# A four-layer graph network on one core: weight generation in six single-bank PSUM places, y copied by halves of nodes, planes loaded one step earlier

## The chip, the cores and the metric

The kernel runs on one core of one Trainium2 chip. The metric is device time in microseconds (us) for one execution; the lower the better. Engine names are those of the profile: PE is TensorE's matmul, PEld its weight load, DVE is VectorE, ACT is ScalarE, POOL is GpSimd, SP is SyncE. Here SP does nothing but start transfers (DMAs); POOL and ACT start some too.

## The reference, cut to what matters

`x` is (8, 2048, 64), `adj` a row-normalised 2048 x 2048 matrix. Four layers each add their result to x after a layer norm and a ReLU. The change lies in and just behind layer 0, a graph convolution whose weights are made for each node from a 16-long embedding:

```python
w = jnp.einsum('nd,dkio->nkio', embedding, weight)   # D = 16, K = 3, 64 x 64 weights for each of 2048 nodes
b = jnp.einsum('nd,do->no', embedding, bias)
As = [I, A, 2.0 * (A @ A) - I]
x_g = jnp.einsum('knm,bmc->bnkc', jnp.stack(As, 0), x)
out = jnp.einsum('bnki,nkio->bno', x_g, w) + b
...
x = x + _L0_gnn_ref(h, adj, ...)          # layer 0
x = x + _L1_gnn_ref(relu(layernorm(x)))   # layer 1: three steps of v -> W2 relu(W1 [v, A v] + b1) + b2
...                                       # layer 2: A x and a linear map; layer 3: attention, done here as a mean
```

## The kernel before, in words

**Stages.** The adjacency matrix is loaded and kept in SBUF (`BT`), and layer 0's terms A h and A A h are formed by matmuls (`bv` in the profile). Then A's chunks are given up for space, except three of sixteen. What follows is the group stage, from about 280 us to 530 us of the span. Behind it A is loaded again (`load_again`, from a bf16 copy), and layers 1 to 3 run, again as `bv` matmuls.

**The group stage** goes over 16 groups `g` of 128 nodes, each in six steps `i`. In step `i` of group `g` the kernel writes, in this order:

- `make_w(g + 1, i)` (line 1160): a sixth of the next group's weights. Sixteen matmuls with 64 contraction rows each (eight pieces `o` of 128 columns, for two row halves `r`) fill two PSUM tiles; then DVE copies the first tile and ACT the second into `w` in SBUF. Group 0's weights are made ahead of the loop, with three `bv` matmuls of the last term of A A h behind each of the six steps.
- `apply_w(g, i)` (line 1246): a sixth of the products y of group g. Steps 0 and 3 open a tile `yb` of two banks and issue 64 short matmuls into it; steps 1, 2, 4 and 5 issue 32 each. Behind steps 2 and 5 the tile is copied to `ys`, half by ACT and half by DVE. There is one `yb` place, so the 64 matmuls of step 0 or 3 write where the previous half of y has just been copied out. After step 5 POOL starts four stores `yD<-ys`.
- `beside(g, i)` (line 1334): pieces of layer 1's first input, for 512 nodes in each round of four groups. `x1_pieces` (line 1276) is a generator with ten pieces; `beside_at` (line 1315) names the ten steps of a round in which they are issued. The last five are: two half copies to planes `pl` (ACT), the second with a store `hp<-pl` from POOL; two transposing loads `pt<-hp` from SP (`load_planes`, line 228); and two joins `gT<-pt` by ACT. One tile `pt` is held.
- `beside_first` (line 1320): some loads for the next round.

At the start of each group SP issues `load_group` for the next one (three transfers, 1 MB), which wait until the group before has released the tile.

**Order.** In this part `nc.on` holds all five engines (line 1055): each engine takes its instructions in the order in which the program writes them, and an instruction that waits holds up all behind it on that engine.

**PSUM.** It has eight banks of 512 fp32 columns. In the loop two pools share them: `psumg` with two `gen` tiles of two banks, and `psumy` with one `genx` tile of two banks and one `yb` tile of two banks. `gen_tile` takes every third tile from `genx`, so there are three generation places of two banks, used in turn, two in each step. Ahead of the loop, while four banks hold other sums, only the two `gen` tiles exist.

**Behind the loop.** `first_operand` makes the three first operands of layer 1 from the joined planes (`bn_u`), and `first_step` (line 1578) runs A times them with four running sums in two tiles of two banks. For m = 0 to 11 it goes over all four sums; then for each sum `nb` it issues the last four chunks, scales the sum on DVE (`g<-bv,crow`), and behind the third one maps the first two results (`bn`), whose PSUM tile takes the place of one of the two sum tiles.

All matmul calls and most others pass through one wrapper, so the profile gives line 67 for nearly everything; groups are told apart by tile names. `w<-gen` is the copy of generated weights, `gen<-E,wg` the generating matmul, `yb<-w,t` the 64 and `yb<-w,tt` the 32 matmuls of y, `ys<-yb` y's copies.

Of the kernel before, what the change touches and what calls it, by code (L numbers as in the profile page):

```python
# [8 lines left out]
F32 = mybir.dt.float32  # L9
# [66 lines left out]
def uniform_path(  # L76
# [42 lines left out]
    psums = [pro.enter_context(tc.tile_pool(name="psump", bufs=1, space=bass.MemoryType.PSUM))]  # L119
# [30 lines left out]
    def bank(tag, name):  # L150
        return psums[-1].tile([P, 512], F32, tag=tag, name=name)
# [221 lines left out]
    def to_feat(h, out, name):  # L373
        pt = transposed(lambda t: h[:, t, :], name)
        nc.scalar.copy(out, pt.rearrange("p t n -> p (t n)"))
        return out
# [305 lines left out]
    ps = bank("b1", f"bv_{nm}")  # L682
    for m in range(NCH):
        if m in (2, 7, 12):
            go_back(1 + m // 5)
        for i in range(2):
            nc.tensor.matmul(
                ps, hls[1][m // 4][i][:, m % 4, :], bt(m)[:, 3 * 512:],
                start=(m == 0 and i == 0), stop=(m == NCH - 1 and i == 1),
# [8 lines left out]
        name="psumt", bufs=2, space=bass.MemoryType.PSUM, reuse_waits="tile"  # L698
# [77 lines left out]
    two = (slice(0, C), slice(C, P))  # L776
# [269 lines left out]
    for m in range(NCH):  # L1046
        i = m if m < 9 else m + 3
# [8 lines left out]
    for n, (kind, p) in enumerate(rounds):  # L1056
        own = kind == "a"
        for nb in range(NB if n + 1 < len(rounds) else 0):
            i = 4 * n + nb
# [8 lines left out]
            if i < 19:  # L1068
                load_ahead(i + 1)
            act(i, -1)  # L1070
            t = product(
                hl_of[kind, p], nb, nm, term(1 if own else 2, f"t{2 - own}T_{nm}"), crows_t[nb],
                fill=fill,
            )
# [8 lines left out]
    psums.pop()  # L1083
    pgs, pls = ExitStack(), ExitStack()
    psg = pgs.enter_context(tc.tile_pool(
        name="psumg", bufs=2, space=bass.MemoryType.PSUM, reuse_waits="tile"
    ))
    psgs.append(psg)
    psl = pls.enter_context(tc.tile_pool(
        name="psuml", bufs=1, space=bass.MemoryType.PSUM, reuse_waits="tile"  # L1090
    ))
    multiply = nc.tensor.matmul
# [35 lines left out]
    wg = wp.tile([P, 2, K * D * C], F32R, tag="A", name="wg")  # L1128
    w1s = [wp.tile([P, P, C], F32, tag="BC"[i], name=f"w1_{i}") for i in range(2)]
    w2 = wp.tile([P, P, C // 2], F32, tag="D", name="w2")  # L1130
# [18 lines left out]
        for hf in range(2):  # L1149
            nc.sync.dma_start(t2s[g % 2][two[hf]], TD[:, 2, :, cs].rearrange("b i n -> i b n"))  # L1150

    gens, moved, pys = [], {}, []

    def gen_tile(g, i, h):
        pool = psg if not pys or len(gens) % 3 < 2 else psums[-1]
        tag = "gen" if pool is psg else "genx"
        gens.append(pool.tile([P, 2, 512], F32, tag=tag, name=f"gen_{g}_{i}_{h}"))
        return gens[-1]

    def make_w(g, i):  # L1160

        e = es_[g]
        ps = [gen_tile(g, i, h) for h in range(2)]
        k2 = i > 3
        n0 = 8 * (i - 4 if k2 else i)
        for o in range(8):
            q, n = divmod(n0 + o, D // 2 if k2 else D)
            at = 2 * D * C * k2 + n * P
            wide = 1 + (g % 4 == 1 and o % 4 < 3)
            for r in range(2):  # L1170
                rs = two[r]
                multiply(
                    ps[r].rearrange("p a f -> p (a f)")[:, o * P:(o + wide) * P],
                    wg[rs, q, at:at + P], e[rs, None, :].to_broadcast([2 * D * 2, wide, P]),
                    start=True, stop=True,
                )
        w, per = (w2, D) if k2 else (w1s[g % 2], 2 * D)
        for h in range(2):
            src = ps[h].rearrange("p a f -> p (a f)").rearrange("p (o n) -> p n o", o=8)
            moved[h] = (nc.vector.tensor_copy, nc.scalar.copy)[h](  # L1180
                w[:, :, per * h + n0:per * h + n0 + 8], src
            )

    load_e(0)
    load_e(1)
# [2 lines left out]
    for k in range(6):  # L1188
        make_w(0, k)
        nb = 1 + k // 2  # L1190
        for q in range(3 * (k % 2), 3 * (k % 2) + 3):
            m, i = order_l[NCH - KEEP + q // 2], q % 2
            multiply(
                lasts[nb], hl[m // 4][i][:, m % 4, :], bt(m)[:, nb * 512:(nb + 1) * 512],
                start=False, stop=(q == 5),
# [16 lines left out]
        name="psumy", bufs=1, space=bass.MemoryType.PSUM, reuse_waits="tile"  # L1212
# [3 lines left out]
    yps, yss = {}, {}  # L1216

    def apply_k(g, u, k):

        T, s_ = divmod(u, 2)  # L1220
        yp, tt, t2 = yps[g, T], tts[g % 2], t2s[g % 2]
        wa = w1s[g % 2].rearrange("p (j q) o -> p q j o", j=4)
        wb = w2.rearrange("p (j q) o -> p q j o", j=4)

        def one(hf, t, par, lhsT, rhs, start, stop):

            q_ = D * hf + 8 * T + 4 * s_ + t
            at = (2 * hf + s_) * P
            multiply(
                yp[32 * t:32 * t + 32, par, at:at + P],  # L1230
                lhsT.rearrange("p b (j q) -> p (b j) q", j=4)[:, :, q_], rhs[:, q_],
                start=start, stop=stop,
            )

        for hf in range(2):
            if k == 0:
                for par in range(2):
                    for t in range(4):
                        one(hf, t, par, tt, wa[:, :, :, 32 * par:32 * par + 32], False,
                            hf == 1 and s_ == 1)  # L1240
                continue
            for t in range(4):
                for par in range(2):
                    one(hf, t, par, t2[two[par]], wb[two[par]], hf == 0 and s_ == 0, False)

    def apply_w(g, i):

        T = i // 3
        if i in (0, 3):
            pool, tag = (psg, "gen") if (g, T) == (NCH - 1, 1) else (psums[-1], "yb")  # L1250
            yps[g, T] = pool.tile([P, 2, 512], F32, tag=tag, name=f"yb_{g}_{T}")
        u = 2 * T
        if i % 3 == 0:
            apply_k(g, u, 1)
            apply_k(g, u + 1, 1)
        else:
            apply_k(g, u + i % 3 - 1, 0)
        if i in (2, 5):
            if T == 0:
                yss[g] = typ0.tile([P, 2, 4, 4 * C], F32, tag="ys", name=f"ys_{g}", bufs=2)  # L1260
            ys, yp = yss[g], yps[g, T]
            for par in range(2):
                (nc.scalar.copy, nc.vector.tensor_copy)[par](
                    ys[:, :, 2 * T:2 * T + 2, :].rearrange(
                        "p h s (j r o) -> p h (s j) r o", j=4, r=2
                    )[:, :, :, par],
                    yp[:, par].rearrange("p (h x o) -> p h x o", h=2, o=32),
                )
            if T == 1:
                nb, t = divmod(g, 4)  # L1270
                yr = ys.rearrange("(x j) h u f -> j x h u f", j=4)
                yd = yD[nb][:, :, :, t].rearrange("t b (j h u) c -> j (t b) h u c", h=2, j=4)
                for j in range(4):
                    nc.gpsimd.dma_start(yd[j], yr[j][:, :, :, j * C:(j + 1) * C])

    def x1_pieces(p, nb, acc, yt, bn):
# [35 lines left out]
                    nc.scalar.copy(out_[:, 0:1], ivt)  # L1312
            yield

    beside_at = [(1, i) for i in (0, 1, 3, 4)] + [(2, i) for i in (0, 1, 3)] + [
        (3, i) for i in (0, 3, 4)
    ]
    firsts_ = []

# [42 lines left out]
    for g in range(NCH):  # L1362
# [28 lines left out]
        name="psum", bufs=2, space=bass.MemoryType.PSUM, reuse_waits="tile"  # L1391
# [186 lines left out]
    def first_step(hl, gT, crow_of, g_new, hl_new, nm, map_two, maps_two, finish_two, scale, add):  # L1578

        two_ = [psums[-1].tile([P, 2, 512], F32, tag="big", name=f"bv2_{i}") for i in range(2)]  # L1580
        sums = [two_[nb // 2][:, nb % 2] for nb in range(NB)]

        def crow(nb):
            crow_of[nb] = load_crow(nb, f"{nm}_{nb}")

        crow(0)
        crow(1)
        for m in range(3 * NB):
            for nb in range(NB):
                chunks(sums[nb], hl, nb, (m,))  # L1590
            if m == KEEP:
                x1_add(last_z.append)
                widen(10, nc.vector.tensor_copy)
                go_on()
                widen(11, nc.vector.tensor_copy)
                go_on()
                for k in range(12, NCH):
                    widen(k, nc.scalar.copy if k in by_act else nc.vector.tensor_copy)
            if m == 2 * NB:
                map_two(0)  # L1600
        ops[0][1].append(to_feat(last_z[0], feat(0, "gT_1_0_3"), "gT_1_0_3"))
        first_operand(3)
        x1_load(1, 0)
        for _ in range(3):
            test_load()
        for nb in range(NB):
            chunks(sums[nb], hl, nb, range(3 * NB, NCH))
            scale(sums[nb], nb)
            if nb < 2:
                crow(nb + 2)  # L1610
            if nb == 2:
                map_two(2)
                finish_two(0, maps_two(0))
            add(nb)
            go_on()
        x1_load(1, 1)
        nc.on = ("gpsimd",)
        first_done.append(products[-1])
        later.extend((x1_behind, x1_behind))

        def put_off():
            ps = maps_two(2)
            return lambda: finish_two(2, ps)

        carry.append(put_off)
        return hl_new, g_new
# [741 lines left out]
```

## Time and profile before

| | |
|---|---|
| time, median of 6 runs | 1152.16 us (1149.37 to 1155.42) |
| profiled execution: time / span | 1148.28 us / 1146.2 us |
| busy share: PE, PEld, DVE, ACT, POOL | 94%, 76%, 56%, 37%, 24% |
| granted TensorE clock, mean | 0.984 |
| `w<-gen` copies, 128 x 1024: DVE x96, ACT x96 | 1221 ns, 1025 ns each |
| `ys<-yb` copies, 128 x 512: DVE x32, ACT x32 | 691 ns, 586 ns each |
| group stage: first `gen` matmul, first `bv` matmul behind it | 279.65 us, 532.22 us |

The two times of the profiled execution differ by 2.1 us, which lie around the span. A line of the timeline gives start, duration, engine, operation, tiles and, in brackets, how long the engine had been idle and who released it. Matmuls overlap, and their durations hold their pipeline; what a burst of matmuls costs is better read from its start to the start of the burst behind it.

### The profile page before, as it was taken

The numbers are of one execution on the slowest core, as the hardware profiler recorded it, in microseconds if no ns is written. First come the engines' busy times: TensorE is split into PE (matmuls) and PEld (weight loads), VectorE is DVE, ScalarE is ACT, GpSimd is POOL, SyncE is SP. The second block draws the span as 40 slices with busy tenths as digits, with TensorE's granted clock in tenths as the row PEclk, the third lists the DMA queues.
The fourth block names the chain that finished last, engine by engine and source line by source line (L and its number), as shares of the span: only waits on it lengthen the run. The fifth ranks groups of instructions, "written<-read, shape, count | busy, mean of one in ns | idle before, by whom it ended". The sixth has DMA issues, their size and how long they took to land.

```text
span 1146.2 us, 27894 instructions
## 1 busy us (share of the span) xinstructions
PE 1081.1 (94%) x12030; PEld 865.6 (76%) x12030; DVE 637.3 (56%) x1096; ACT 429.1 (37%) x594; POOL 276.0 (24%) x313
## 2 busy tenths in 40 slices
PE   9999999999999999997898988999799999899996
PEld 7778788887788888886676765776577777688875
DVE  5555434411656666663586567557755644556575
ACT  5814322431445555554434432353244323211110
POOL 6514100100122313131123343134313300332121
PEclk9999999999999999999999999999899999899998
DMA  9936567555544454548697467736883663431432
GB/s 350 388 113 171 176 180 178 171 156 180 129 97 119 107 127 116 129 127 283 131 196 205 112 174 193 170 108 153 200 177 102 183 131 84 151 108 47 141 112 77
DMA packets 160196, 179.28 MB, mean 156 GB/s; under 512 B 63048, under 2 KB 114888, under 8 KB 157504
## 3 DMA queue, kind: packets, MB, share of 16 engines
q1 hardware_dynamic: 139744, 116.99, 41.5%
q0 software_dynamic: 13760, 45.21, 11.9%
q10 hardware_dynamic: 6560, 15.21, 4.1%
q8 instruction: 96, 1.57, 0.6%
q14 instruction: 36, 0.29, 0.1%
HBM read 111.81 MB, written 53.22 MB: 144 GB/s over the span
## 4 chain that ended last, share of the span: by engine, by line
PE 63%; DMA 11%; DVE 9%; issue 5%; ACT 5%; POOL 3%; SPq 2%; ACTq 0%; DVEq 0%; POOLq 0%
PE bv L67 28%; PE gen L67 5%; PE yb L67 5%; PE bv_2a L67 3%; PE bv_3a L67 3%; DMA yD<-ys 2%; PE bv_1a L67 2%; PE bv_2b L67 2%; PE bv_1b L67 2%; PE bv_0b L67 2%; PE bn L67 2%; PE bv_3b L67 2%; DVE z L67 2%; DVE ys L67 2%; ACT w L67 2%
## 5 line engine op out<-in xcount | busy, mean ns | idle before, releaser
L67 POOL TENSOR_TENSOR rstd<-var,mhalf 128x8 f32<-128x8 f32 x64 | 109.7, 1715 | 302.0 <-DVE var L67 299.2
L67 DVE COPY w<-gen 128x1024 f32<-128x1024 f32 x96 | 117.2, 1221 | 78.8 <-PE gen L67 78.8
L67 ACT COPY w<-gen 128x1024 f32<-128x1024 f32 x96 | 98.4, 1025 | 122.2 <-PE gen L67 122.2
L67 PE MATMUL gen<-E,wg 64*128 64x128 f32 (+1 forms) x1536 | 123.4, 282 | 1.3 <-ACT w L67 1.3
L67 PEld LDWEIGHTS gen<-E,wg 64*128 64x128 f32 x1536 | 104.7, 186 | 23.0 <-issue 8.4
L67 ACT ACTIVATE sq<-z 128x512 f32<-128x512 f32 x64 | 40.5, 632 | 197.1 <-DVE z L67 143.8
L67 POOL DMA_DIRECT2D yD<-ys x64 | 37.3, 590 | 176.2 <-DVE ys L67 174.5
L67 PE MATMUL yb<-w,tt 128*32 128x128 f32 x2048 | 73.7, 283 | 3.9 <-issue 3.9
L67 PE MATMUL bv<-BT_C,H 128*128 128x512 f32 x192 | 77.1, 401 | 0.0
L67 PE MATMUL bv<-BT_B,L 128*128 128x512 f32 x192 | 76.2, 397 | 0.2 <-DVE L L67 0.2
L67 PE MATMUL bv<-BT_B,H 128*128 128x512 f32 x192 | 75.9, 395 | 0.0
L67 PE MATMUL bv<-BT_C,L 128*128 128x512 f32 x192 | 75.8, 395 | 0.0
L67 DVE SCALAR_TENSOR_TENSOR z<-z,rstd 128x512 f32<-128x512 f32 x64 | 44.7, 698 | 50.5 <-POOL rstd L67 49.9
L67 PEld LDWEIGHTS yb<-w,tt 128*32 128x32 f32 x2048 | 59.5, 166 | 9.3 <-issue 4.9
L67 PE MATMUL bv<-BT,H 128*128 128x512 f32 x144 | 59.4, 413 | 3.2 <-ACT H L67 3.2
L67 DVE TENSOR_TENSOR g<-bv,crow 128x512 f32<-128x512 f32 x48 | 32.9, 686 | 52.4 <-PE bv L67 52.4
L67 PE MATMUL bv<-BT_A,L 128*128 128x512 f32 x144 | 57.0, 396 | 1.1 <-DVE L L67 1.1
L67 PE MATMUL bv<-BT,L 128*128 128x512 f32 x144 | 57.3, 398 | 0.5 <-DVE L L67 0.5
L67 PE MATMUL bv<-BT_A,H 128*128 128x512 f32 x144 | 56.6, 393 | 0.0
L67 DVE SCALAR_TENSOR_TENSOR junk<-mt,cols,st 128x512 uint8<-128x512 bf16 x64 | 47.7, 746 | 10.4 <-DMA mt<-MD 10.0
L67 POOL TENSOR_TENSOR acc<-acc,wl 128x512 f32<-128x512 f32 x16 | 21.5, 1342 | 126.5 <-DVE z L67 125.8
L67 DVE SCALAR_TENSOR_TENSOR z<-mean,acc 128x256 f32<-128x256 f32 x112 | 50.2, 486 | 1.4 <-DMA hs<-z 0.5
(271 smaller groups left out, 2381.5 us busy)
## 6 DMA issues: line engine op xcount, KB each, us to landing
BT<-in_adj_dram POOLq DMA_DIRECT2D x16, 1024.0 KB, 12.3
crow<-crowD SPq DMA_DIRECT2D x64, 256.0 KB, 3.5
st<-in_adj_dram SPq DMA_DIRECT2D x64, 256.0 KB, 4.5
MD<-md ACTq DMA_DIRECT2D x16, 512.0 KB, 4.2
tt<-TD SPq DMA_DIRECT2D x16, 512.0 KB, 4.4
t<-TD SPq DMA_DIRECT2D x32, 256.0 KB, 5.8
xs<-acc POOLq DMA_DIRECT2D x32, 256.0 KB, 3.1
acc<-xs SPq DMA_DIRECT2D x32, 256.0 KB, 3.6
```

The source lines that it names most:

```text
L67: made = f(*args, **how)
```

## The change

It has four parts.

1. The generation tiles are of one bank instead of two: four `gen` and two `genx` places. `make_w` takes its eight pieces in two halves `a` of four; behind each half it copies two tiles of 512 columns, one by DVE and one by ACT. Ahead of the loop there are four places instead of two.
2. In groups with `g % 2 == 1` instead of `g % 4 == 1`, three of four generating matmuls stream 256 columns instead of 128; the second 128 columns are overwritten by the next matmul.
3. y is copied by halves of nodes (`h`), ACT the first and DVE the second, where each engine took one bank (`par`) before. For the very last half of y, two single-bank tiles stand in for one of two banks, and there are four copies of 256 columns. In `first_step` the sums 0 and 2 now share a tile, and 1 and 3, where 0 and 1 did, and 2 and 3.
4. The ten pieces are issued at other steps: `load_planes` in step 4 of a round's third group instead of step 0 of its fourth, and the two joins in steps 1 and 3 instead of 3 and 4.

```diff
@@ psumg
-        name="psumg", bufs=2, space=bass.MemoryType.PSUM, reuse_waits="tile"
+        name="psumg", bufs=4, space=bass.MemoryType.PSUM, reuse_waits="tile"
@@ gen_tile, make_w
-    def gen_tile(g, i, h):
-        pool = psg if not pys or len(gens) % 3 < 2 else psums[-1]
-        tag = "gen" if pool is psg else "genx"
-        gens.append(pool.tile([P, 2, 512], F32, tag=tag, name=f"gen_{g}_{i}_{h}"))
+    def gen_tile(g, i, h, a):
+        pool = psg if not pys or len(gens) % 6 < 4 else psums[-1]
+        tag, bufs = ("gen", 4) if pool is psg else ("genx", 2)
+        gens.append(pool.tile([P, 512], F32, tag=tag, name=f"gen_{g}_{i}_{h}_{a}", bufs=bufs))
...
-        ps = [gen_tile(g, i, h) for h in range(2)]
-        for o in range(8):
-            q, n = divmod(n0 + o, D // 2 if k2 else D)
-            wide = 1 + (g % 4 == 1 and o % 4 < 3)
+        for a in range(2):
+            ps = [gen_tile(g, i, h, a) for h in range(2)]
+            for o in range(4):
+                q, n = divmod(n0 + 4 * a + o, D // 2 if k2 else D)
+                wide = 1 + (g % 2 == 1 and o < 3)
...
+            for h in range(2):
+                o0 = per * h + n0 + 4 * a
+                (nc.vector.tensor_copy, nc.scalar.copy)[h](
+                    w[:, :, o0:o0 + 4], ps[h].rearrange("p (o n) -> p n o", o=4)
                 )
@@ apply_w
-            for par in range(2):
-                (nc.scalar.copy, nc.vector.tensor_copy)[par](
-                    ys[:, :, 2 * T:2 * T + 2, :].rearrange(
-                        "p h s (j r o) -> p h (s j) r o", j=4, r=2
-                    )[:, :, :, par],
-                    yp[:, par].rearrange("p (h x o) -> p h x o", h=2, o=32),
-                )
+            for h in range(2):
+                copy = (nc.scalar.copy, nc.vector.tensor_copy)[h]
+                to = ys[:, h, 2 * T:2 * T + 2, :].rearrange("p s (j r o) -> p r (s j) o", j=4, r=2)
+                if len(yp) == 3:
+                    copy(to, yp[2].rearrange("p r (h x o) -> p h r x o", h=2, o=32)[:, h])
+                    continue
+                for r in range(2):
+                    copy(to[:, r], yp[r].rearrange("p (h x o) -> p h x o", h=2, o=32)[:, h])
@@ beside_at
-    beside_at = [(1, i) for i in (0, 1, 3, 4)] + [(2, i) for i in (0, 1, 3)] + [
-        (3, i) for i in (0, 3, 4)
+    beside_at = [(1, i) for i in (0, 1, 3, 4)] + [(2, i) for i in (0, 1, 3, 4)] + [
+        (3, i) for i in (1, 3)
     ]
@@ first_step
-        sums = [two_[nb // 2][:, nb % 2] for nb in range(NB)]
+        sums = [two_[nb % 2][:, nb // 2] for nb in range(NB)]
```

More of the change, by code (lines that the diff above doesn't have):

```diff
@@ L1150, in load_group @@
             nc.sync.dma_start(t2s[g % 2][two[hf]], TD[:, 2, :, cs].rearrange("b i n -> i b n"))
-    gens, moved, pys = [], {}, []
-    def gen_tile(g, i, h):
-        pool = psg if not pys or len(gens) % 3 < 2 else psums[-1]
-        tag = "gen" if pool is psg else "genx"
-        gens.append(pool.tile([P, 2, 512], F32, tag=tag, name=f"gen_{g}_{i}_{h}"))
+    gens, pys = [], []
+    def gen_tile(g, i, h, a):
+        pool = psg if not pys or len(gens) % 6 < 4 else psums[-1]
+        tag, bufs = ("gen", 4) if pool is psg else ("genx", 2)
+        gens.append(pool.tile([P, 512], F32, tag=tag, name=f"gen_{g}_{i}_{h}_{a}", bufs=bufs))
         return gens[-1]
@@ L1162, in make_w @@
         e = es_[g]
-        ps = [gen_tile(g, i, h) for h in range(2)]
         k2 = i > 3
         n0 = 8 * (i - 4 if k2 else i)
-        for o in range(8):
-            q, n = divmod(n0 + o, D // 2 if k2 else D)
-            at = 2 * D * C * k2 + n * P
-            wide = 1 + (g % 4 == 1 and o % 4 < 3)
[L1170 to L1175, printed above, removed]
-                )
[L1177 to L1181, printed above, removed]
-            )
+        w, per = (w2, D) if k2 else (w1s[g % 2], 2 * D)
+        for a in range(2):
+            ps = [gen_tile(g, i, h, a) for h in range(2)]
+            for o in range(4):
+                q, n = divmod(n0 + 4 * a + o, D // 2 if k2 else D)
+                at = 2 * D * C * k2 + n * P
+                wide = 1 + (g % 2 == 1 and o < 3)
+                for r in range(2):
+                    rs = two[r]
+                    multiply(
+                        ps[r][:, o * P:(o + wide) * P],
+                        wg[rs, q, at:at + P], e[rs, None, :].to_broadcast([2 * D * 2, wide, P]),
+                        start=True, stop=True,
+                    )
+            for h in range(2):
+                o0 = per * h + n0 + 4 * a
+                (nc.vector.tensor_copy, nc.scalar.copy)[h](
+                    w[:, :, o0:o0 + 4], ps[h].rearrange("p (o n) -> p n o", o=4)
+                )
     load_e(0)
@@ L1229, in one @@
             multiply(
-                yp[32 * t:32 * t + 32, par, at:at + P],
+                yp[par][32 * t:32 * t + 32, at:at + P],
                 lhsT.rearrange("p b (j q) -> p (b j) q", j=4)[:, :, q_], rhs[:, q_],
@@ L1249, in apply_w @@
         if i in (0, 3):
-            pool, tag = (psg, "gen") if (g, T) == (NCH - 1, 1) else (psums[-1], "yb")
-            yps[g, T] = pool.tile([P, 2, 512], F32, tag=tag, name=f"yb_{g}_{T}")
+            if (g, T) == (NCH - 1, 1):
+                yps[g, T] = [
+                    psg.tile([P, 512], F32, tag="gen", name=f"yb_{g}_{T}_{par}") for par in range(2)
+                ]
+            else:
+                yb = psums[-1].tile([P, 2, 512], F32, tag="yb", name=f"yb_{g}_{T}", bufs=1)
+                yps[g, T] = [yb[:, 0], yb[:, 1], yb]
         u = 2 * T
@@ L1261, in apply_w @@
             ys, yp = yss[g], yps[g, T]
-            for par in range(2):
-                (nc.scalar.copy, nc.vector.tensor_copy)[par](
-                    ys[:, :, 2 * T:2 * T + 2, :].rearrange(
-                        "p h s (j r o) -> p h (s j) r o", j=4, r=2
-                    )[:, :, :, par],
-                    yp[:, par].rearrange("p (h x o) -> p h x o", h=2, o=32),
-                )
+            for h in range(2):
[4 more added lines that the diff above has]
+                    continue
+                for r in range(2):
+                    copy(to[:, r], yp[r].rearrange("p (h x o) -> p h x o", h=2, o=32)[:, h])
             if T == 1:
```

## The prediction

> **What bounds the kernel now.** The page comes first: PE is busy for 94% of the span, and the rows of the groups show both copy engines idle most of the time before a copy, waiting for PE. So the question is what PE's own bursts wait for. The timeline of a plain stretch of the group stage (half of group 10) answers it:
>
> ```profile
> 439.95 1.31 PE L67 MATMUL gen<-E,wg 64*128 64x128 f32 x16
> 440.07 0.58 ACT L67 COPY ys<-yb 128x512 f32<-128x512 f32 x1
> 440.69 0.69 DVE L67 COPY ys<-yb 128x512 f32<-128x512 f32 x1 [0.58 <-ACT ys L67]
> 441.43 1.25 PE L67 MATMUL yb<-w,t 64*32 64x128 f32 x64 [0.17 <-DVE ys L67]
> 442.62 1.11 PE L67 MATMUL gen<-E,wg 64*128 64x128 f32 x16
> 443.66 1.15 PE L67 MATMUL yb<-w,tt 128*32 128x128 f32 x32
> 443.76 1.22 DVE L67 COPY w<-gen 128x1024 f32<-128x1024 f32 x1 [0.66 <-PE gen L67]
> 444.73 1.41 PE L67 MATMUL gen<-E,wg 64*128 64x128 f32 x16
> 446.08 1.14 PE L67 MATMUL yb<-w,tt 128*32 128x128 f32 x32
> 447.15 0.33 PE L67 MATMUL gen<-E,wg 64*128 64x128 f32 x1
> ```
>
> From start to start, a generation burst takes 1.04 us where nothing holds it (442.62 to 443.66), 1.35 at 444.73 and 1.48 at 439.95. The burst of 444.73 writes the place that DVE empties from 443.76 to 444.98: 0.25 us late, the missing 0.31 with a semaphore's delay. The 1.48 has another cause: the 64 y matmuls behind it need `yb` empty, and its copies run one after the other, ACT to 440.65, DVE to 441.38, PE at 441.43. A half group is thus 1.19 (64 y) + 1.04 + 1.07 + 1.35 + 1.07 + 1.48 = 7.20 us, a group 14.41 (starts of the 64 at 324.48 and 338.89). In a doubled group the free burst is 1.08 (354.50 to 355.58) and the group 14.59 (353.31 to 367.90).
>
> Then the chain that ended last, at the end of the stage:
>
> ```profile
> 516.01 11.87 DMA pt<-hp
> ...
> 528.54 0.58 ACT ys L67
> ...
> 529.14 0.52 DVE ys L67
> ...
> 529.75 0.69 DVE L_u L67
> ```
>
> The planes, issued at 514.74 behind seven 512 KB loads of A, hold ACT (8.26 us idle before the first join); behind ACT wait the last y copy and the first operands, so PE has no `bv` matmul before 532.22, though y's matmuls began their last burst at 521.77.
>
> **The change part by part.**
>
> *Six places.* With places of one bank taken in order, half a burst needs the copy of three halves before. At 444.73 that copy would be long over, so 1.35 becomes 1.04: 0.31 a half group. The new copies have 512 columns; I price them by y's, which are that size and also from PSUM: 691 ns on DVE, 586 on ACT. DVE then has 12 x 0.69 + 2 x 0.69 = 9.7 us in a plain group, and 12.3 in the group with the most pieces (11.3 busy now, + 12 x 0.69 - 6 x 1.22 = 1.0), against a period of 13.8. The first half's copy starts half a burst earlier, so y's copies find DVE free as now. Bounds: no gain if a small copy costs 1.0 us (rival d); 0.4 a half if every burst gets the 0.97 that the weight loads take.
>
> *Doubling.* The free burst costs 0.04 more; the one ahead of y's wait nothing. Eight groups instead of four.
>
> Plain periods become 14.41 - 0.62 = 13.79, doubled ones 13.79 + 4 x 0.04 = 13.95. Fifteen periods generate: now 11 x 14.41 + 4 x 14.59 = 216.9; after 7 x 13.79 + 8 x 13.95 = 208.1. **Sum: -8.8** (-5 to -12).
>
> *Ahead of the loop* six bursts with three `bv` matmuls each take 2.32 (284.27 to 286.60 is 2.33), and PE waits 0.21 for ACT's copy with the burst stretched besides. Free, it is 1.04 + 3 x 0.23 = 1.73; DVE needs as much (four copies of 0.69 and one scaling of 0.68 in two bursts: 1.72 each). With both this close I take 1.87: **-2.7** (-1.5 to -3.5).
>
> *y by halves.* I count nothing. The old copies read different banks of one tile and yet ran one after the other. That this is a rule of reading one PSUM tile, not of what is written, is shown where ACT and DVE take different parts of a tile `wt`:
>
> ```profile
> 165.41 0.75 DVE L67 TENSOR_SCALAR wst<-wt,rows 128x512 f32<-128x512 f32 x1 [4.57 <-DMA MD<-md]
> 166.20 0.59 ACT L67 CAST whq<-wt 128x512 fp32r<-128x512 f32 x1 [2.69 <-DVE wst L67]
> ```
>
> ACT needs nothing that DVE makes there, and starts 0.04 us behind it. The new halves still share the tile, so 1.48 stays. The four small copies of the very last half overlap in part; that is 0.2 us and not counted. Bounds: 0, and -0.44 a half group if they do run together (a rival). The Trainium skill (PSUM — Partial Sum Buffer, "PSUM bank collisions raise a hardware error") has it that two engines may not be in one bank and partition quadrant at once, two readers included, but may be in different banks. The trace is stricter than that on the old copies (0.58 us idle across banks); on the new ones, which both read both banks, page and trace agree on no overlap.
>
> *Planes earlier.* Two transposing loads move on SP ahead of `load_group` (three transfers) in the rounds' third groups, and of `load_again` (seven) at the end. SP will stand there for the store `hp<-pl` (issued 508.23, 2.5 us to landing), then 2 x 1.25 us of issue; `load_group` has a period of 14 us to land in 4.4 to 5.9, and A's first reloaded chunk is used 5.5 us into `bv`: both hidden, 2.5 us if not. On ACT the joins pass ahead of two steps of copies; landing by 4.2 us (median of `pt`) puts the first at 15.4 to 16 us from its group's start, the join's place is at 17: no stall; with 7.3 us as at 398.12 some 1.4 us, which three half-burst places cover.
>
> At the end the planes land near 516 instead of 527.9. From 513.73 to 523.27 PE does y (its 2.94 us pause with no releaser kept); then two operands (2.05), the third behind the first one's release (`L_u`, about 2.5 behind y), 1.1 more: `bv` starts 13.1 us from 513.73, now 18.5. **-5.5** (-2 to -8.5, the pause gone too).
>
> *Sums in other pairs.* The same tile rule shows here:
>
> ```profile
> 562.58 0.50 PE L67 MATMUL bv<-BT_C,H_u 128*128 128x512 f32 x1 [0.78 <-DVE g L67]
> 567.37 1.11 PE L67 MATMUL bn<-wl,g 64*64 64x64 f32 x64
> 568.89 0.68 DVE L67 TENSOR_TENSOR g<-bv,crow 128x512 f32<-128x512 f32 x1
> 569.63 0.51 PE L67 MATMUL bv<-BT_C,H_u 128*128 128x512 f32 x1 [1.16 <-DVE g L67]
> ```
>
> Sums 1 and 3 wait for the scaling of 0 and 2. Those waits go (-0.8, -1.2). But `bn` takes the tile of sums 0 and 2 and must now wait for the scaling at 568.89, which DVE reaches late because a test waits 1.40 for its transfer: `bn` moves 2.2 us back, and with it PE's last sum and the operands for the next step. **+0.5** (-0.8 to +1.5).
>
> **Sum:** -8.8 - 2.7 - 5.5 + 0.5 = -16.5. From the profiled 1148.28 us that is 1131.8; that execution lay 3.9 under the median, so from 1152.16 it is **1135.7**.
>
> **Rivals.**
> (a) *y's copies do run together.* For it: all written parts are separate blocks now, interleaved before. Against: `wst`/`whq` above. The 64 matmuls would wait only for the 1.04 burst: 2 x 15 x 0.44 = -13.2, and doubling costs 0.04 more in 16 bursts: about -13 further, 1122.5.
> (b) *Only the generation gains*: planes land late behind other traffic (11.9 us once already), `bn` loses 1.5, the start gives 1.5: -8.8 - 1.5 + 1.5 = about -9: 1143.
> (c) *No change*: PE is held for the copies as before, if half bursts are released together. Against: each tile has its own two copies. 1152.
> (d) *Slower: DVE becomes the bound.* 384 copies replace 192, and a fixed part is paid twice; runs of four elements are written instead of eight. In four periods DVE has 48 copies of d, eight y copies (5.5) and 4.3 us of pieces (4 x 0.68, 0.75, 0.85 in the timeline of groups 4 to 7); this reaches the present 57.6 us at d = 1.0. At 1.1 the period is 15.65, +18.6 over 15, less 5.5 at the end: 1165. Against: 691 ns for the same size.
>
> **How the numbers follow.** Chances: forecast 0.57, (a) 0.16, (b) 0.12, (c) 0.05, (d) 0.10. A difference of 0.3% (3.5 us) is about what can be told here. Faster: 0.57 + 0.16 + 0.12 = 0.85; same 0.05; slower 0.10. The forecast's own range by its terms is 1128 to 1144; with (a) at the low end and (b) at the high one I give 1119 to 1147, which leaves out (c), (d) and the far side of (a).
>
> **What would show it.** Right: `w<-gen` x192 on each engine near 690 and 590 ns; unheld bursts of 1.04 everywhere but ahead of the 64, where 1.48 and DVE's idle for ACT stay; a period near 13.8; no `pt<-hp` in the chain at the end, `bv` within 4 us behind y; PE's wait at the second sum gone, one before `bn` in its place. Wrong: copies of 1.0 us or more with DVE busy throughout; DVE's y copy starting with ACT's; ACT idle for `pt` in every fourth group.

## The result, and the profile after

The changed kernel takes 1146.07 us (median of 36 runs, 1140.37 to 1155.87) against 1154.61 us of the kernel before (78 runs beside them). The ratio is 0.9944, 95% interval 0.9931 to 0.9956: some 6.5 us faster, where 16.5 were forecast. The ratio is taken over undisturbed executions alone, while the median of 1154.61 holds some with a lower granted clock, so the two medians lie further apart (8.5 us) than the gain. Beside it on another chip, in the experiments below, the same kernel gave 0.9926 (0.9893 to 0.9959). The profiled execution took 1141.99 us with a span of 1140.3 us at a granted clock of 0.984.

The group stage went nearly as forecast. Two rows of the costliest groups (operation, shapes, count | busy us, mean ns | idle us before, and its releaser):

```profile
L67 DVE COPY w<-gen 128x512 f32<-128x512 f32 x192 | 123.5, 685 | 52.8 <-PE gen L67 52.2
L67 ACT COPY w<-gen 128x512 f32<-128x512 f32 x192 | 104.2, 595 | 94.3 <-PE gen L67 93.6
```

The small copies cost what the forecast took from y's copies (691 and 586 ns), and both engines still wait for PE and not the other way round. The timeline of half of a group:

```profile
452.37 0.59 ACT L67 COPY ys<-yb 128x512 f32<-128x512 f32 x1 [0.45 <-PE yb L67]
...
452.98 0.69 DVE L67 COPY ys<-yb 128x512 f32<-128x512 f32 x1 [0.93 <-ACT ys L67]
...
453.73 1.26 PE L67 MATMUL yb<-w,t 64*32 64x128 f32 x64 [0.44 <-DVE ys L67]
...
457.02 1.11 PE L67 MATMUL gen<-E,wg 64*128 64x128 f32 x16
...
458.06 1.15 PE L67 MATMUL yb<-w,tt 128*32 128x128 f32 x32
459.13 1.15 PE L67 MATMUL gen<-E,wg 64*128 64x256 f32 x16
...
460.63 1.25 PE L67 MATMUL yb<-w,t 64*32 64x128 f32 x64 [0.34 <-DVE ys L67]
```

The burst that took 1.35 us from start to start takes 1.04 (457.02 to 458.06); only the one ahead of the 64 is still held (459.13 to 460.63, 1.50), because DVE's y copy still begins when ACT's ends. From the first `gen` to the last it is now 221.40 us (278.27 to 499.67), before 231.31; the last `gen` starts 11.3 us earlier, of which 1.4 us are there at the first one.

At the end of the stage the planes are loaded in time, so the 5.16 us of waiting shrink to 0.51:

```profile
509.80 1.58 PE L67 MATMUL yb<-w,tt 128*32 128x128 f32 x47 [2.33 <-issue]
513.87 1.16 PE L67 MATMUL bn_u<-w1e,gT 128*128 128x128 f32 x8 [0.51 <-DVE L_u L67]
```

The first `bv` behind them starts at 514.78 us, before at 532.22: **17.4 us earlier**, where the steps up to there had summed to 17.0. Yet the span is only 5.9 us shorter. So what has to be found is where 11.5 us went *behind* the first `bv`, in a stretch of the program that the change touches in one line.

Two places show. First, the fourth operand of `first_step`. The timeline of the kernel before has one line for the last load of x1 (`yt`, DVE adds it):

```profile
541.40 0.69 DVE L67 TENSOR_TENSOR acc<-acc,yt 128x512 f32<-128x512 f32 x1 [2.59 <-DMA yt<-yD]
```

and the kernel after:

```profile
526.75 0.69 DVE L67 TENSOR_TENSOR acc<-acc,yt 128x512 f32<-128x512 f32 x1 [5.47 <-DMA yt<-yD]
...
541.38 0.66 PE L67 MATMUL pt_gT<-ident,z 128*128 128x128 f32 x4 [3.12 <-ACT gT L67]
```

Counted from its own first `bv`, `yt` came 9.2 us in and now comes 12.0 us in. Behind it on DVE stand the widenings of the reloaded chunks `BT_C`, behind those ACT's casts and copies, and PE has nothing to do for 3.12 us. What was in front of `yt` shows in SP's own lines (SPq, which starts the transfers), first of the kernel before, then of the change:

```profile
523.47 2.28 SPq L67 DMA_DIRECT2D BT_C<-MD  x4
525.96 2.27 SPq L67 DMA_DIRECT2D BT_D<-MD  x2
537.12 2.55 SPq L67 DMA_DIRECT2D yt<-yD  x4
```

```profile
511.46 2.40 SPq L67 DMA_DIRECT2D BT_C<-MD  x4
514.84 1.83 SPq L67 DMA_DIRECT2D BT_D<-MD  x2
520.26 2.54 SPq L67 DMA_DIRECT2D yt<-yD  x4
```

SP issues `yt` when y's last stores have landed; it waits for `yD<-ys` 8.6 us in the kernel before and 3.3 us in the change. Before, these stores hung on the late planes, and 13.65 us lay between the first issue of C and that of `yt`. Now it is 8.80 us, and C and D, which take 9.2 and 9.7 us to land (medians of their issues), are still on their way: the DMA share is 0.97 or more in every 2 us from 508 to 526.

Behind the idle the granted clock falls to a half, from 543 until 550; in windows of 2 us (PE busy and count, PEld, DVE, ACT, POOL, clock, DMA share, GB/s):

```profile
540.00:542.00 2.00, 0.62 (x4) 0.42 (x4) 0.00 (x0) 1.88 (x4) 0.00 (x0) 1.00 0.00 0
...
544.00:546.00 2.00, 1.32 (x4) 0.59 (x4) 0.69 (x1) 0.58 (x1) 0.00 (x0) 0.50 0.00 0
```

Second, the new pairing of the sums. These lines answer to the fourth fence of the prediction:

```profile
555.29 0.75 DVE L67 SCALAR_TENSOR_TENSOR junk<-mt,cols,st 128x512 uint8<-128x512 bf16 x1 [1.19 <-DMA mt<-MD]
...
555.97 0.68 DVE L67 TENSOR_TENSOR g<-bv,crow 128x512 f32<-128x512 f32 x1
556.19 1.41 PE L67 MATMUL ph<-g,wl 64*64 64x512 f32 x2 [1.89 <-ACT gT L67]
556.71 2.59 PE L67 MATMUL bn<-wl,g 64*64 64x64 f32 x64
...
559.39 1.23 DVE L67 TENSOR_TENSOR bn<-bn,wl 128x1024 f32<-128x1024 f32 x1 [2.74 <-PE bn L67]
```

The two waits at the sums (0.78 and 1.16 us) are gone, as forecast. But `bn` waits for the scaling of sum 2 at 555.97, which stands behind a test that waits for its transfer; PE is idle for 1.89 us, returns at half clock, and `bn` takes 2.59 us where it took 1.11. (What ends the idle time is the next step's `ph<-g`, which now stands ahead of `bn` on PE and waits for one of ACT's copies; `bn` itself starts 0.06 us behind the end of that scaling, 556.65.)

### The profile page after: what moved, and what is told of

Same layout as the page of the kernel before. It is cut to its first block, busy times and chain, and to the rows that moved or that the text cites. A ratio compares the mean times of both kernels' runs of the same rounds, so it can differ in the third digit from the quotient of the medians.

```text
span 1140.3 us, 28137 instructions
## 1 busy us (share of the span) xinstructions
PE 1070.9 (94%) x12030; PEld 859.2 (75%) x12030; DVE 645.0 (57%) x1193; ACT 435.1 (38%) x691; POOL 275.2 (24%) x313
## 3 DMA queue, kind: packets, MB, share of 16 engines
q0 software_dynamic: 13760, 45.21, 11.9%
## 4 chain that ended last, share of the span: by engine, by line
PE 61%; DMA 11%; DVE 11%; issue 6%; ACT 5%; SPq 3%; POOL 3%; ACTq 0%; DVEq 0%; POOLq 0%
PE bv L67 22%; PE yb L67 8%; PE gen L67 5%; SPq L67 3%; PE bv_2a L67 3%; PE bv_3a L67 3%; PE bv_1a L67 3%; PE bv_2b L67 2%; PE bv_0a L67 2%; DMA yt<-yD 2%; DVE z L67 2%; PE bv_3b L67 2%; PE bv_1b L67 2%; DVE ys L67 2%; DMA hp<-pl 2%
## 5 line engine op out<-in xcount | busy, mean ns | idle before, releaser
L67 DVE COPY w<-gen 128x512 f32<-128x512 f32 x192 | 123.5, 685 | 52.8 <-PE gen L67 52.2
L67 ACT COPY w<-gen 128x512 f32<-128x512 f32 x192 | 104.2, 595 | 94.3 <-PE gen L67 93.6
L67 PE MATMUL gen<-E,wg 64*128 64x128 f32 (+1 forms) x1536 | 109.0, 281 | 0.5 <-issue 0.5
L67 PEld LDWEIGHTS gen<-E,wg 64*128 64x128 f32 x1536 | 94.7, 186 | 17.4 <-issue 8.9
## 6 DMA issues: line engine op xcount, KB each, us to landing
BT<-in_adj_dram POOLq DMA_DIRECT2D x16, 1024.0 KB, 12.4
```

What stands on the lines that cost most here:

```text
L67: made = f(*args, **how)
```

## The experiments

**Theory A:** the 17.4 us are there at the first `bv`, and are lost in `first_step` at these two places: the pairing of the sums, and `yt` late behind the reloads of C and D. **Theory B:** something further back (transfers, VectorE's chain) sets the end, so that nothing that is won here reaches it.

To see where time is won or lost, each PE matmul of a run is set beside the same one of the kernel before, counted from the end, and the starts are subtracted. Each cell is from one profiled execution; the clock falls now and then in the group stage too (to 0.50 from 370 to about 383 us in the old-sums run), so the column that tells causes apart is the fourth, the difference of the two to its left. Two profiles of one kernel differ by up to 3 us in it (the change 11.8 and 8.9). The place "622" is the matmul that starts at 622 us in the kernel before, some 50 us behind `first_step`.

| kernel | first `bv` | at 622 | lost between | end | ratio of times, 95% |
|---|---|---|---|---|---|
| the change | -17.4 | -5.6 | 11.8 | -6.2 | 0.9944 (0.9931-0.9956) |
| the change again (c_after) | -14.3 | -5.4 | 8.9 | +1.8 | 0.9926 (0.9893-0.9959) |
| old sums (e1) | -9.0 | -4.2 | 4.8 | -2.0 | 0.9887 (0.9834-0.9939) |
| yt first (e2) | -12.4 | -4.6 | 7.8 | -2.9 | 0.9900 (0.9865-0.9935) |
| old sums, yt first (e5) | -10.3 | -8.2 | 2.1 | -3.2 | 0.9879 (0.9839-0.9919) |
| the same again (c_e5) | -13.8 | -12.7 | 1.1 | -7.8 | 0.9857 (0.9809-0.9906) |
| new sums, tests behind (e12) | -16.1 | -14.1 | 2.0 | -12.5 | 0.9897 (0.9853-0.9941) |
| e12 and yt first (e14) | -15.7 | -16.5 | -0.8 | -12.4 | 0.9857 (0.9800-0.9914) |
| before, new sums alone (e6) | +1.0 | +6.1 | 5.1 | +10.7 | 1.0110 (1.0048-1.0171) |
| before, planes and yt first (e13) | -5.7 | -4.6 | 1.1 | -3.2 | 0.9940 (0.9911-0.9970) |
| old planes (e3) | -2.6 | +3.4 | 6.0 | +7.7 | 0.9950 (0.9917-0.9983) |
| six places alone (e4) | -9.9 | -8.2 | 1.7 | -2.6 | 0.9891 (0.9831-0.9951) |
| the change, y as before (e7) | -8.1 | -0.6 | 7.5 | +4.2 | 0.9943 (0.9915-0.9971) |
| e5, doubling as before (e8) | -15.8 | -11.9 | 3.9 | -9.9 | 0.9852 (0.9810-0.9893) |
| e5 with old planes (e10) | -5.6 | -4.7 | 0.9 | -2.4 | 0.9930 (0.9893-0.9967) |

**The sums.** Old pairing in the changed kernel:

```diff
-        sums = [two_[nb % 2][:, nb // 2] for nb in range(NB)]
+        sums = [two_[nb // 2][:, nb % 2] for nb in range(NB)]
```

> The changed kernel with the old pairing of the sums in the first step (one sum's bn, then its scaling and bv, as before). Theory A: of the 17.4 us by which the first bv comes earlier, about 3 us are lost because bn now stands behind the scaling of two sums; with the old pairing they come back: ratio to the kernel before about 0.9915 against 0.9944 of the change, with the waits of 0.78 and 1.16 us for the scaling back in the trace and the 1.9 us idle before the next step's product gone. Theory B (the end is set further back by transfers and VectorE, so nothing won here reaches it): ratio 0.994, the same as the change.

Measured 0.9887: better than the 0.9915 that A expected, by its median; the interval is wide. 4.8 us are lost between the two places where the change loses 8.9 and 11.8, though the clock is at a half from 550.6 to 560.8, behind a wait of 1.95 us for the late `yt` before `pt_gT`. The same line of the change put alone into the kernel before:

> The kernel before with only the new pairing of the sums in the first step. Forecast: +0.5 us, ratio 1.0004. Theory A: +3 to +5 us, ratio 1.003 to 1.004, with bn behind the scaling of sum 2 and the next step's first product ahead of it on TensorE. Theory B: 1.000.

Measured 1.0110 (1.0048 to 1.0171): slower by 5.5 us or more at the interval's lower end, where even A expected 3 to 5. The forecast's +0.5 is refuted. (Of the 5.1 us in its row, 1.1 stand ahead of the sums, where the clock is at a half from 533.2 to 536.6; some 4 are left.) The timeline shows the same sequence, in a kernel in which nothing else is changed:

```profile
570.04 0.75 DVE L67 SCALAR_TENSOR_TENSOR junk<-mt,cols,st 128x512 uint8<-128x512 bf16 x1 [1.28 <-DMA mt<-MD]
...
570.58 1.85 PE L67 MATMUL ph<-g,wl 64*64 64x512 f32 x2 [2.05 <-ACT gT L67]
...
570.72 0.69 DVE L67 TENSOR_TENSOR g<-bv,crow 128x512 f32<-128x512 f32 x1
...
571.47 2.67 PE L67 MATMUL bn<-wl,g 64*64 64x64 f32 x64
...
574.23 1.23 DVE L67 TENSOR_TENSOR bn<-bn,wl 128x1024 f32<-128x1024 f32 x1 [2.82 <-PE bn L67]
```

`bn`'s result reaches DVE at 574.23 where it did at 569.50: 4.7 us later, though the sums themselves were 1 us late only. Some 45 us further on, x1's next load is used late too (2.55 us of waiting at 616.32, before 0.69 at 608.42), and the second half of an operand stands behind it on DVE.

That it is this order, and not the pairing as such, is shown by moving the two tests that belong to sum 1 behind the scaling of sum 2, in the changed kernel:

```diff
             scale(sums[nb], nb)
...
             if nb == 2:
+                held()                      # the two tests of sum 1
                 map_two(2)
                 finish_two(0, maps_two(0))
-            add(nb)
+            held = add(nb, nb != 1)         # returns the tests instead of issuing them
             go_on()
```

> The changed kernel, new pairing kept, with the two tests that belong to sum 1 moved on VectorE from ahead of the scaling of sum 2 to behind it. Theory A (the new pairing costs because bn waits for that scaling, which stands behind a test that waits 1.3 us for its transfer, and TensorE then idles about 2 us and comes back at half clock): the scaling is 2 to 3 us earlier, TensorE's idle there under 0.7 us, bn 1.1 us long instead of 2.6, and of the pairing's price two thirds come back: ratio 0.989 to 0.991. Rival (the price lies elsewhere, as in later waits for the tile): 0.9926 to 0.9944, like the change.

Measured 0.9897 (0.9853 to 0.9941), which is A's 0.989 to 0.991 by its median, with an interval that reaches the rival's 0.9926 to 0.9944; the trace tells them apart: only 2.0 us are lost between the two places. The timeline:

```profile
550.88 0.68 DVE L67 TENSOR_TENSOR g<-bv,crow 128x512 f32<-128x512 f32 x1
...
551.66 1.16 PE L67 MATMUL bn<-wl,g 64*64 64x64 f32 x64 [0.27 <-issue]
...
553.13 0.75 DVE L67 SCALAR_TENSOR_TENSOR junk<-mt,cols,st 128x512 uint8<-128x512 bf16 x1 [0.91 <-DMA mt<-MD]
```

PE stands still for 0.27 us, the clock stays at 1.00, `bn` takes 1.16 us, and the test that waits for its transfer now holds up only the step behind `bn`, by about 1 us. The sums' two old waits are gone as well, and `bn` runs ahead of the next step's `ph<-g` again.

**yt and the planes.** (The expectations also call C and D, the reloaded chunks of A, planes.) In the changed kernel, one load put ahead of the reloads:

```diff
+            x1_rest(0, NB - 1, *firsts_.pop(0))
             load_again("C", 4)
             load_again("D", 2)
-            x1_rest(0, NB - 1, *firsts_.pop(0))
```

> The changed kernel with the tail's load of yt (x1's rest, all but the last blocks) issued ahead of the reloads of planes C and D. Theory A: yt lands before the planes, GpSimd and VectorE are through with x1 before they widen C and D, the 3.1 us idle of TensorE before pt_gT goes and the granted clock stays near 1.00 there (0.50 in the change): ratio about 0.9915. If the planes then come late instead: bv of C waits for its reload by up to 4 us and the ratio stays 0.994 to 0.996. Theory B: 0.994.

Measured 0.9900 (0.9865 to 0.9935), a little better than A's 0.9915. `yt` is used 7.7 us behind the first `bv` instead of 12.0, and no wait for `gT` precedes `pt_gT` any more. 7.8 us are still lost, as the new pairing is still there. SP now stands at `yt` until y's stores have landed (10.6 us), so C is issued behind it, at 525.85. The reloads come late for DVE by 0.69 and 1.20 us, but not for PE, whose longest wait there is 0.68 us as before. One part of the expectation failed: the clock still falls to a half, from 547.4 to 550.8.

The price of the late `yt` stands out at `pt_gT` (556.05 in the kernel before). Counted in the same way from the first `bv` to there, the five profiles (e9's left out) with the planes earlier and `yt` behind the reloads lose 2.8, 1.4 (the change and its second run), 1.6 (e1), 1.3 (e7) and 1.0 us (e12); the six with `yt` first (e2, both of e5, e8, e13, e14) win 0.5 each.

Then the place of the planes; in the changed kernel it is put back:

```diff
-    beside_at = [...] + [(2, i) for i in (0, 1, 3, 4)] + [(3, i) for i in (1, 3)]
+    beside_at = [...] + [(2, i) for i in (0, 1, 3)] + [(3, i) for i in (0, 3, 4)]
```

> The changed kernel with the planes loaded where they were loaded before (at the last half group's y), everything else as in the change. The forecast's sum: 5.5 us lost, ratio 0.999. Theory A: the first bv comes 4.5 to 6 us later, but the reloads get back the time that they lack ahead of it, so the wait before pt_gT goes and the end moves by 0 to 2 us: ratio 0.994 to 0.996. Theory B: 0.994.

Measured 0.9950 (0.9917 to 0.9983), what A expected; against 0.9944 and 0.9926 of the whole change the earlier planes bring 1 to 3 us there by the medians, with overlapping intervals. Its profile also shows the new pairing's wait once more, but with the clock at 1.00:

```profile
565.89 1.07 PE L67 MATMUL ph<-g,wl 64*64 64x512 f32 x2 [2.06 <-ACT gT L67]
566.87 1.16 PE L67 MATMUL bn<-wl,g 64*64 64x64 f32 x64
```

From `pt_gT` to the next step's first `bv` (572.69 in the kernel before) this profile loses nothing, e6 and e7 1.4 us each; to 580 it is 1.3 against 2.7. So about half of the price there is the half clock. It rests on one profile. The same lines the other way round, alone in the kernel before:

> The kernel before with only the planes loaded just behind the store. Forecast's term: -5.5 us, ratio 0.9952, no pt in the chain at the end of the group stage. Theory A: the first bv comes 4 to 5.5 us earlier, then TensorE waits for the planes' widening before pt_gT with its clock at a half, and 0 to 3 us are left: ratio 0.997 to 1.000.

Measured 0.9983 (0.9952 to 1.0013), within A's range; its profile, at a granted clock of 0.935, isn't used. With yt ahead of the reloads as well:

> The kernel before with the planes loaded just behind the store and yt ahead of the reloads; nothing else of the change. Theory A (planes alone, 0.9983, lose what they win because yt lands late behind the reloads): the forecast's 5.5 us are there, ratio 0.995 within 0.002, with no wait for gT before pt_gT. Rival (the end is bound further back): 0.998, like the planes alone.

Measured 0.9940 (0.9911 to 0.9970), which is A's number and below B's 0.998, though the intervals of the two runs touch. The first `bv` comes 5.7 us earlier, 4.6 are left at 622, and the line that was 5.47 us of waiting in the change reads:

```profile
534.29 0.69 DVE L67 TENSOR_TENSOR acc<-acc,yt 128x512 f32<-128x512 f32 x1 [1.20 <-DMA yt<-yD]
```

**Both together**: the one-line edits of the old sums and of yt, in the changed kernel.

> The changed kernel with both repairs: the old pairing of the sums, and yt loaded ahead of the reloads of planes C and D. Theory A (the gain is there at the first bv and is lost in two places in the first step, some 3 us each with the clock that falls behind the idle): both come back, ratio 0.984 to 0.988, and from the first bv to sum 3's bv the kernel is as quick as the one before. Theory B (the end is set further back): same ratio as the changed kernel beside it, within 0.002.

> The kernel with both repairs (old pairing of the sums, yt ahead of the reloads) once more, as the one that the two beside it are to be compared with. Theory A, now that the new pairing alone measured 1.011: ratio 0.986 within 0.004, near the forecast's 0.9857 for the parts that it had priced as gains (-16.5 us of 1152) and well under the change's 0.9926 to 0.9944.

Measured 0.9879 (0.9839 to 0.9919) and 0.9857 (0.9809 to 0.9906), and 2.1 and 1.1 us lost between the two places (3.9 in e8 below, the same kernel but for the doubling). By the medians this kernel is quicker than with either edit alone, with intervals that overlap; both intervals lie below the 0.9931 to 0.9956 of the change and overlap that of its second run (0.9893 to 0.9959) a little. With the old `beside_at` in it:

> That kernel with the planes loaded where they were loaded before. Forecast's term: 5.5 us lost, ratio 0.0048 higher than the one beside it, the first bv about 19 us behind the last gen instead of 14 to 15. Theory A (part of what the planes win at the first bv is lost behind it, where the stretch of the next half is bound by VectorE's and the DMA's chain): 1 to 3 us, ratio 0.001 to 0.003 higher.

Measured 0.9930 (0.9893 to 0.9967): 0.0073 or 8 us more than the one beside it, the intervals overlapping, nearer to the forecast's 5.5 us than to A's 1 to 3. In the profiles the first `bv` is 15 to 17 us behind the last `gen` with the planes moved and 21.8 without, and what is lost up to 622 is the same (1.1 and 0.9): with both repairs the planes' term stays whole that far, and A's expectation was too low. Last, both repairs with the new pairing kept:

> The changed kernel with the new pairing kept, the two tests of sum 1 behind the scaling of sum 2, and yt ahead of the reloads. Theory A: both losses are mended, and of the pairing its saved waits are left (0.8 and 1.2 us): ratio 0.983 to 0.988, at or just under the version with the old pairing (0.9879 and 0.9857). Rival (the gains of the two repairs are one and the same): 0.990, like either alone.

Measured 0.9857 (0.9800 to 0.9914). It loses nothing between the two places (-0.8 us), so by the profiles the two losses add; whether it beats the old pairing can't be told from these intervals.

**The other parts.** Of the change only `make_w` and the places:

> Of the change only the six places of one bank in the generation (with the start ahead of the loop that goes with them); sums, planes, doubling and the copies of y as before. The forecast's terms added: -8.8 -2.7 = -11.5 us, ratio 0.990, better than the whole change (Theory A: nothing at the tail is pressed together, so the whole of it reaches the end). Theory B: 0.994, as the end is set by something that no longer moves.

Measured 0.9891 (0.9831 to 0.9951), A's 0.990: by the median the six places alone bring more than the whole change did, though the intervals overlap.

```diff
-            for h in range(2):                      # nodes' halves, each of both banks
-                copy(to, yp[2].rearrange(...)[:, h])
+            for par in range(2):                    # one bank each
+                copy(ys...[:, :, :, par], yp[par]...)
```

> The changed kernel with y copied by par again (one whole half-par by ScalarE, the other by VectorE, both from the two tiles of 512 columns). Forecast and Theory A: the copies follow one another either way, so nothing changes: ratio within 0.001 of the changed kernel beside it, TensorE's wait for VectorE's ys some 0.3 to 0.8 us per half group in both. Rival (a), copies by halves of nodes run side by side: the changed kernel gains up to 0.4 us per half group from them, 32 half groups, so without them the ratio is 0.008 to 0.012 higher.

Measured 0.9943 (0.9915 to 0.9971) beside 0.9926 of the change on that chip: no difference that can be told, and 0.008 to 0.012 is outside. The groups in the window from 280 to 500 us, first of the change, then of this kernel:

```profile
L67 DVE COPY ys<-yb 128x512 f32<-128x512 f32 x29 | 20.0, 691 | 27.9 <-ACT ys L67 27.9
```

```profile
L67 DVE COPY ys<-yb 128x512 f32<-128x512 f32 x28 | 19.4, 692 | 27.9 <-ACT ys L67 27.9
```

DVE's copy waits for ACT's in both, 27.9 us in all.

```diff
-                wide = 1 + (g % 2 == 1 and o < 3)
+                wide = 1 + (g % 4 == 1 and o < 3)
```

> That kernel with the doubled columns in every fourth group, as before, instead of every second. Forecast: four groups at 4 x 0.04 us less, 0.6 us, no difference that can be told (ratio within 0.002 of the one beside it). Rival: doubling is there for the granted clock; without it the clock in the group stage falls below 1.00 in some profiled window, and the time is 3 us or more longer (ratio 0.003 higher).

Measured 0.9852 (0.9810 to 0.9893) beside 0.9857: nothing that can be told, and the granted clock is 1.00 from the first `gen` to the last in both.

The change itself, unaltered:

> The changed kernel once more, unaltered, so that it stands on the same chip as the three beside it. Both theories: ratio to the kernel before 0.9944 within 0.003; the group stage (first gen to last gen) 221.4 us within 1 us unless the granted clock falls in it, and the first bv of the tail 12 us behind the last gen.

Measured 0.9926 (0.9893 to 0.9959). First to last `gen` takes 223.05 us, 1.65 more than in the first profile with the clock at 1.00 throughout, so the expected 1 us was too narrow; the first `bv` 17 us behind the start of the last `gen` (the expected 12 was counted wrongly: in the first profile it is 15.1).

**What stays open.** Behind 622 the offsets to the kernel before still slip, by -0.6 to 7.2 us, also in kernels whose later part is the one before (e4: 5.6, e6: 4.6, e10: 2.3). The profiled execution of the kernel before lay 3.9 us under its median, and the falls of the clock at 690, 810 and 990 us differ from profile to profile. How much of the slip is chance and how much is bound there wasn't settled; B is right for that part at most. What decides whether the half clock follows a wait, as it does at `bn` in five profiles of six (not in e3), wasn't tried either.

## Why the prediction was right, and where it was wrong

Forecast 1135.7 us, measured 1146.07, within the range and on the right side, but 16.5 us of gain against 6.5. The reference is not the reason: the ratio puts the kernel before at 1152.5 us beside it, and the forecast had 1152.16. Two terms failed, the cover of the earlier planes and the new pairing of the sums.

- *Six places and the start ahead of the loop* (-8.8 and -2.7): the mechanism is right, the size a little high. From the first `gen` to the last it is 9.9 us less, against 11.5: 2.4 ahead of the loop (first `gen` to the first 64 of y, 12.66 after 15.09) and 7.6 in the fifteen periods (211.44 after 218.99; the prediction counted 208.1 after 216.9, as if all were plain or doubled, but in both kernels two take about 15 us). That the last `gen` starts 11.3 us earlier, and the first `bv` 17.4 where 17.0 were summed, is in part luck: the first `gen` already starts 1.4 us earlier, and over all profiles it starts anywhere from 277.0 to 282.5. Bursts of 1.04 and copies of 685 and 595 ns are as worked out. Rival (d), DVE as the bound, is out: DVE waits 52 us for PE in these copies.
- *Doubling* (eight periods at 0.04 more per free burst): right within what can be told; a doubled period is 13.97 us (319.99 to 333.96), forecast 13.95.
- *y by halves* (0): right, and rival (a) is out. The rule in the prediction, one reader of a PSUM tile after the other, held for the old and the new split. By the Trainium skill's rule on banks (PSUM — Partial Sum Buffer, "PSUM bank collisions raise a hardware error") the old split could have run side by side; in e7, with it put back, the copies again did not.
- *Planes earlier* (-5.5): the term was right up to the first `bv` (-5.7 measured in e13), and so was "no `pt<-hp` in the chain". The step that failed is the sentence on cover, "A's first reloaded chunk is used 5.5 us into `bv`: both hidden, 2.5 us if not". It asked who waits for the chunk that is moved, and A's first chunk indeed kept no one waiting. It did not ask what else the wait for the planes had covered. `yt` stands behind the reloads in SP's queue and needs y's last stores, which had waited for the planes too; that gave C and D the 13.65 us in which they landed. With 8.80 us they are still on their way, and `yt` is used 6.5 us after its issue (520.26 to 526.75) instead of 4.3 (537.12 to 541.40). The price was 1.0 to 2.8 us at `pt_gT`; up to 622, where the clock falls differently from profile to profile, nothing to 4 us (11.8, 8.9 and 7.5 lost against 7.8; 4.8 against 2.1, 1.1 and 3.9; 2.0 against -0.8).
- *Sums in other pairs* (+0.5, -0.8 to +1.5): the mechanism was named, its size was too small by some eight times. Measured alone it is some 4 us at 622, and 1.0110 by time. The term set 2.2 us of a later `bn` against 2.0 us of saved waits. Of the saved waits only the first came through (0.9 us at sum 1, alone in the kernel before); PE then stood still ahead of `bn` for 1.89 to 2.06 us, and in five of six profiles the half clock followed, so that `bn` itself took about 1.5 us more (2.59 for 1.11). The bound of +1.5 held no price for an idle PE other than the idle time. In e3, the sixth, the half clock stays away and nothing is lost up to the next step: there the term's sum of waits holds, and 1.3 us are lost in the step behind it.
- *The sum as such*: it carried every microsecond won at the first `bv` to the end. For the six places that holds (1.7 us lost on the way to 622 in e4); for what shifts against the transfers in flight it doesn't.

Rival (b), "Only the generation gains", gave 1143 and is the nearest in number, but for another reason: the planes weren't late, and the pairing lost more than twice the 1.5 us that `bn` was given.

## What to carry to other kernels

A wait that is taken away on one engine is worth its length only if the engine has work to do then; look for the place where it stands still next, and add what the granted clock may lose behind it. A wait also gives the transfers in flight time to land: before taking it away, see which loads are issued behind it and what would then still be in front of them. And where an instruction comes to depend on a result of an in-order engine, read what else stands ahead of that result there: two tests with a late transfer, moved by one place, undid most of the loss.

## What the runs showed of the hardware

An idle time of TensorE well under 3 us was enough for the half clock, but did not bring it every time. Behind 1.89 us in the change (554.3 to 556.2) the granted clock was 0.50 from 556.8 to 560.2; behind 3.12 us in the change, and behind 1.73 us at the same place in its second run, both with few matmuls around them, it was 0.50 for 6.8 us. Behind 2.06 us in e3, 1.63 us in e7 and 1.36 us in e12 it stayed at 1.00. In e2, where two waits of 0.68 us are all that is left at `pt_gT`, it fell all the same (547.4 to 550.8), and in the kernel before, with the same two waits, it didn't. So the length of one idle time does not decide it here. The Trainium skill (TensorE: Matmul & The Clock Gate, "What's actually happening") puts the fall behind at least one idle window of about 3.4 us and the return behind one busy window of that length. The length of the half clock agrees (3.4 us, and twice that); the idle time that sufficed was shorter here than the page has it.
